# Layer 0's cross-attention: one weighted sum over two steps of scores instead of one per step, and where the third tile of exps is kept

## The chip, the cores and the metric

The kernel runs on one core of a Trainium2 chip. The metric is the device time of one execution in microseconds (us); lower is better. Five engines work side by side, each through its own list of instructions in order, and wait for each other by semaphores: TensorE (PE in the profile; its weight loads are listed apart as PEld), VectorE (DVE), ScalarE (ACT), GpSimd (POOL) and SyncE (SP), which here only starts transfers. TensorE writes its results to PSUM; VectorE and ScalarE read them from there.

## What is computed

The whole is a small network of two layers, each with a cross-attention, a second mixer and a feed-forward part. The change touches only the first cross-attention, with 2 sequences of 256 queries, 16 heads of width 16, and 4096 keys per sequence:

```python
def _L0_xattn_ref(x, z, Wq, Wkv, Wo):
    Q = (x @ Wq.T).reshape(B, xN, NUM_HEADS, HEAD_DIM)
    KV = (z @ Wkv.T).reshape(B, zN, 2, NUM_HEADS, HEAD_DIM)
    K = KV[:, :, 0]
    V = KV[:, :, 1]
    attn = jnp.einsum('bqhd,bkhd->bhqk', Q, K) * SCALE
    attn = jax.nn.softmax(attn, axis=-1)
    O = jnp.einsum('bhqk,bkhd->bqhd', attn, V).reshape(B, xN, DIM)
    return O @ Wo.T
```

The self-attention of layer 1, much later, uses two weight maps (`wq`, `wk`) whose place in memory moves with the change.

## The kernel before

All is in float32, which TensorE works off in two passes per matmul. The 16 heads of a sequence are cut into four groups of four heads; with two sequences there are eight groups `G`. The four heads of a group lie in four bands of 32 partitions, so that four score matmuls with 32 rows of contraction can run on TensorE at the same time, each on its own 32 rows of the array.

The softmax needs the largest score of each query, so a group is gone through twice, in 16 steps (`STEPS`) each:

- The first pass (function `first`) puts 128 queries on the partitions and 512 keys along the row, and VectorE takes the maximum along the row (`ve.reduce_max` in `scores`). After 16 steps `greatest` makes the maxima of the group final, and `lowered` writes them, negated, into a spare row of the queries, by a transpose on TensorE (`ps_negm`).
- The second pass (function `second`) puts 128 keys on the partitions and 256 queries along the row, for two blocks of keys per step, and ScalarE takes the exponential into `exps`, a tile in SBUF (`se.activation`).
- The weighted sum (function `weigh`) multiplies these exps with the values `V`. Here the array is used the other way, with 128 rows of contraction and 32 columns per head: four heads side by side on columns. A sum of a step is eight matmuls into one bank of PSUM (`av`), and VectorE adds that bank to an accumulator in SBUF (also named `av`).

The second pass of a group runs `LAG` = 17 steps behind its first pass, so in steps 17 to 127 one step holds both: the first pass of step `n` and the second pass of step `s = n - 17`. Such a step calls `scores` twice. Each call has eight matmuls: two heads of the first pass into one double tile of two banks (`banks`, a ring of two such tiles, `ps2`), and the other two heads of the second pass into two single banks (`bank`, a ring of four, `ps1`). The sums, the keys (`ps_k`), the values (`ps_v`), the transposes of the maxima and the final transposes of a group (`ps_o`, in `finished`) take their banks from the same ring of four. After the two calls comes `weigh` for the step before, and after that what `made` has laid down for this step: every fourth step the projection of another 512 keys and, in most of the stage, of 512 values.

In steps 0 to 16 only the first pass runs, in steps 128 to 144 only the second, mixed there with the first instructions of the next stage.

`in_order` makes the instructions of the engines stand in the order in which the program calls them; from step 17 on nothing is moved by the scheduler within an engine. Loads that are not urgent (`LATE`) are issued on GpSimd's queue, one entry per step from step 20.

The exps live in one tile of 4096 columns (tag `P`), used in two halves in turn (`s % 2`). The maps `a1_wq` and `a1_wk` have tiles of their own, loaded through `LATE`.

Of the kernel before, what the change touches and what calls it, by code (L numbers as in the profile page):

```python
# [10 lines left out]
F32 = mybir.dt.float32  # L11
# [4 lines left out]
P = 128  # L16
B, NQ, D = 2, 256, 256
# [6 lines left out]
E, FF = 8, 1024  # L24
# [18 lines left out]
def perceiver(ctx: ExitStack, tc: tile.TileContext, d: dict, out: bass.AP):  # L43
    nc = tc.nc
# [5 lines left out]
    big = ctx.enter_context(pool("big", 1))  # L50
# [4 lines left out]
    def bank(name):  # L55
        return ps1.tile([P, 512], F32, tag="bank", name=name)
# [7 lines left out]

    def large(tag, name):
        return big.tile([P, 4096], F32, tag=tag, name=name)

# [25 lines left out]
    for j in range(4):  # L95
        nc.gpsimd.memset(one0[32 * j : 32 * j + 1, :], 1.0)
    ctxT = [large(f"ctx{b}", f"ctxT{b}") for b in range(B)]

    def load_ctxT(b, c, eng):
# [6 lines left out]
    load_ctxT(0, 2, nc.sync)  # L106
    load_ctxT(0, 3, nc.sync)
    cols = const.tile([P, 2, d["cols"].shape[1]], F32, tag="cols", name="cols")
    wo0, bcw, gate_w, out_w, x1_wq, x1_wkT, x1_wv, a1_wq, a1_wk, a1_wv, a1_wo, wr = (
        const.tile([P, d[n].shape[0] // P, d[n].shape[1]], F32, tag=n, name=n)  # L110
        for n in (
            "l0_wo", "l0_bcw", "l0_gate_w", "l0_out_w", "x1_wq", "x1_wkT", "x1_wv",
            "a1_wq", "a1_wk", "a1_wv", "a1_wo", "moe_wr",
        )
    )
    bcb = const.tile([P, 2 * NS], F32, tag="l0_bcb", name="l0_bcb")
# [15 lines left out]
    def ctxT1(c):  # L132
# [4 lines left out]
        late(t, (t, d[n].rearrange("(c p) n -> p c n", p=P)))  # L137
        for t, n in (
            (wo0, "l0_wo"), (bcw, "l0_bcw"), (gate_w, "l0_gate_w"), (out_w, "l0_out_w"), (cols, "cols"),
            (x1_wq, "x1_wq"), (x1_wkT, "x1_wkT"), (x1_wv, "x1_wv"), (a1_wq, "a1_wq"), (a1_wk, "a1_wk"),  # L140
            (a1_wv, "a1_wv"), (a1_wo, "a1_wo"), (wr, "moe_wr"),
        )
    ] + [
# [531 lines left out]
    def self_attention(b, bank):  # L675
# [138 lines left out]
        for n in range(NG + 3):  # L814
# [20 lines left out]
            if 0 <= n - 3:  # L835
                weigh(n - 3, pe(n - 3))
# [27 lines left out]
    with pool("l0x", 1) as one:  # L864
# [19 lines left out]
        STEPS = NK // 2  # L884
# [14 lines left out]
        def blank(i, c):  # L899

            nc.scalar.copy(KB[i][:, c * 1024 : (c + 1) * 1024], one0.to_broadcast([P, 1024]))

        KC = {}

        def keys(h2, c):

            b, half = divmod(h2, 2)
            ps = bank("ps_k")
            te.matmul(
                ps, lhsT=wkc[:, half * P : (half + 1) * P], rhs=ctxT[b][:, c * 512 : (c + 1) * 512],  # L910
                start=True, stop=True,
            )
            KC[h2, c] = KCS[(h2 * chunks + c) % 4]
            se.copy(KC[h2, c], ps)
# [69 lines left out]
        def scores(n, ms, s, ss, p):  # L984


            work, done = [], []
            for j, pair in ms:
                G, i = divmod(n, STEPS)
                c, qt = divmod(i, 2)  # L990
                tiles, at = homes(pair)
                work += [(first, n, j + jj, at[jj]) for jj in range(2)]
                for k, t in enumerate(tiles):
                    w = 2 // len(tiles)
                    done.append(
                        lambda t=t, o=MP[G][:, qt, j + k : j + k + w, c]: ve.reduce_max(o, t, axis=AX.X)
                    )
            for j, pair in ss:
                tiles, at = homes(pair)
                work += [(second, s, j + jj, at[jj]) for jj in range(2)]  # L1000
                for k, t in enumerate(tiles):
                    w = 2 // len(tiles)
                    o = p[:, j + k : j + k + w, :] if pair else p[:, j + k, :]
                    done.append(lambda t=t, o=o: se.activation(o, t, AF.Exp))
            for h in range(2):
                for f, *at in work:
                    f(*at, h)
            for f in done:
                f()

        def weigh(n, p):

            G, kp = divmod(n, STEPS)
            b, g = groups[G]
            vt = VT[2 * b + g // 2]
            ps = bank("av")
            for c in range(2):
                for j in range(4):
                    at = (2 * kp + c) * HW + (4 * (g % 2) + j) * VW
                    te.matmul(  # L1020
                        ps[32 * j : 32 * j + 32, :NQ],
                        lhsT=vt[:, at : at + 32],
                        rhs=p[:, j, c * NQ : (c + 1) * NQ],
                        start=(c == 0),
                        stop=(c == 1),
                    )
            if kp == 0:
                AV[G] = one.tile([P, NQ], F32, tag="av", name="av")
                ve.tensor_copy(AV[G], ps[:, :NQ])
            else:  # L1030
                ve.tensor_tensor(AV[G], AV[G], ps[:, :NQ], ALU.add)

        def greatest(G):
            m = small.tile([P, 2, 4], F32, tag="m", name="m")
            ve.reduce_max(m, MP[G], axis=AX.X)
            lowest_of(lambda qt: m[:, qt, :], negm)

        def lowered(G):
            b, g = groups[G]
            lower(QT[g][:, b * NQ : (b + 1) * NQ], negm, bank("ps_negm"))  # L1040

        def finished(G):
            b, g = groups[G]
            ps = bank("ps_o")
            for qt in range(2):
                te.transpose(ps[:, qt * P : (qt + 1) * P], AV[G][:, qt * P : (qt + 1) * P], ident)
            o = ps[:, : 2 * P].rearrange("p (q j r) -> p q j r", q=2, r=32)
            f = small.tile([P, 2, 4], F32, tag="af", name="f")
            ve.reciprocal(f, o[:, :, :, DH])
            ve.tensor_tensor(  # L1050
                O[b][:, :, 4 * DH * g : 4 * DH * (g + 1)].rearrange("p q (j r) -> p q j r", r=DH),
                o[:, :, :, :DH],
                f.unsqueeze(3).to_broadcast([P, 2, 4, DH]),
                ALU.mult,
            )
# [34 lines left out]
            f(*at)  # L1090
        for c in range(4):
            blank(1, c)
        before = None
        closing = None
        for n in range(NM + LAG + 1):
            G, i = divmod(n, STEPS)
            s = n - LAG
            one_pass = n < NM
            other = 0 <= s < NM
            if s == 0:  # L1100
                exps = large("P", "exps")
            p = exps[:, s % 2 * 2048 : (s % 2 + 1) * 2048].rearrange("p (j n) -> p j n", j=4) if other else None
            if one_pass and i == 0:
                MP[G] = small.tile([P, 2, 4, NC // 512], F32, tag="mp", name="mp")
            in_order[0] = other
            if one_pass and other:
                scores(n, [(2, True)], s, [(0, False)], p)
                if i == 0:
                    lowered(G - 1)
                scores(n, [(0, True)], s, [(2, False)], p)  # L1110
            else:
                four = [(2, False), (0, True)]
                if one_pass:
                    scores(n, four, s, [], p)
                elif other:
                    scores(n, [], s, four, p)
                if n and i == 0 and n <= NM:
                    lowered(G - 1)
            if one_pass and i == STEPS - 1:
                greatest(G)  # L1120
            if closing is not None:
                finished(closing)
                closing = None
            if before:
                weigh(*before)
            if before and before[0] % STEPS == STEPS - 1:
                closing = before[0] // STEPS
            before = (s, p) if other else None
            for f, *at in made.get(n, ()):
                f(*at)  # L1130
        if closing is not None:
# [28 lines left out]
        weights.append((w1, w2))  # L1160

    LOADED = len(HOMES)
    xn5 = const.tile([P, NT, D], F32, tag="l0_wq", name="xn5")
    count = const.tile([P, P], F32, tag="l0_wv", name="count")
    nc.gpsimd.iota(count, pattern=[[1, P]], base=1, channel_multiplier=0, allow_small_or_imprecise_dtypes=True)
# [36 lines left out]
    for stream in streams.values():  # L1202
        assert next(stream, None) is None
    for e in range(LOADED):
        experts(e)
# [3 lines left out]
    with pool("ffn", 1) as one:  # L1209
# [83 lines left out]
        two = one.tile([P, TOP_E, NT, E], F32, tag="two", name="two")  # L1293
# [6 lines left out]
        for t in range(NT):  # L1300
            for i in range(TOP_E):
                w = nc.gpsimd.indirect_dma_start(
                    out=x_slots, out_offset=bass.IndirectOffsetOnAxis(ap=at[:, i, t : t + 1], axis=0),
                    in_=xn5[:, t, :], in_offset=None,
# [7 lines left out]
        before = one.tile([P, E - 1, E], F32, tag="before", name="before")  # L1312
# [140 lines left out]
        def next_weights(k):  # L1453
            e = k + LOADED
            if e < ALWAYS:
                experts(e if e < E else expert_of(e))
            if k == STORED - 3:
                shares(STORED)
                shares(STORED + 1)
            if k == STORED - 1:  # L1460
                collect()
# [109 lines left out]
```

## Time and profile before

| | us |
|---|---|
| median of three runs | 868.06 (865.57 to 869.98) |
| the profiled execution | 865.26 |
| its span, first to last instruction | 863.5 |

The profile is of one execution. Its span is 1.8 us shorter than the time of the same execution, and that time is 2.8 us under the median. Most lines of the kernel go through the class `Engine`, so the profile shows them all as line 164, and one has to tell them apart by the names of their tiles: `mp<-ps` are the maxima of the first pass, `exps<-ps` the exponentials of the second, `av<-exps,V` the weighted sums, `av<-av` their additions. In a row of a matmul a count is of passes, two per matmul. "x4" behind a line of the timeline means four instructions merged into one line.

The stage with both passes runs from about 67 us to 445 us. Cut into stretches, engine by engine (busy us, number of instructions), its middle looks the same throughout:

```profile
240.00:280.00 40.00, 40.00 (x582) 26.81 (x582) 30.79 (x35) 27.52 (x53) 0.00 (x0) 1.00 0.08 19
280.00:320.00 40.00, 39.86 (x566) 26.58 (x563) 31.32 (x41) 25.87 (x51) 0.59 (x2) 1.00 0.09 19
320.00:360.00 40.00, 39.96 (x584) 26.85 (x584) 31.51 (x40) 26.44 (x51) 0.00 (x0) 1.00 0.10 22
```

The columns after the stretch and its length are TensorE, its weight loads, VectorE, ScalarE and GpSimd, then the granted clock of TensorE as a share of full speed, the share of the DMA engines and GB/s.

### The profile page before, as it was taken

To read this page: it belongs to the slowest core of one execution; us is meant where nothing else is said; L and a number is where in the kernel's file an instruction comes from. 1 tells how busy PE (TensorE), PEld (TensorE's weight loads), DVE (VectorE), ACT (ScalarE), POOL (GpSimd) and SP (SyncE) were. 2 spreads that over 40 slices of the span, in tenths; PEclk is the share of its full clock that TensorE was granted. 3 is DMA by queue.
4 is the path that set the end of the run, shared out by engine and by line. 5 is a ranking of instruction groups with operands and counts; after the bars stand their busy time and mean duration, and the time that the engine had idled before them with its cause. 6 is when DMAs were issued, how large, how long until landed. Compare 5 with 4: busy or idle time off the path is not lost.

```text
span 863.5 us, 20999 instructions
## 1 busy us (share of the span) xinstructions
PE 814.6 (94%) x8640; PEld 586.5 (68%) x8640; DVE 571.9 (66%) x1044; ACT 458.8 (53%) x858; POOL 46.1 (5%) x108
## 2 busy tenths in 40 slices
PE   5999999999999999999999899878999999699996
PEld 3665666666666666666665478756488866499995
DVE  4788888878787878788863668985743376641112
ACT  6436666766666666666668758621642225411120
POOL 5004020000000000000000000000000000030003
PEclk9999999999999999999999989998999969889999
DMA  7216131011010010000010203000222500529602
GB/s 269 55 32 184 24 115 42 21 23 23 17 23 20 19 23 19 22 19 2 2 51 2 80 19 86 13 1 1 97 98 98 195 1 2 195 70 329 229 20 81
DMA packets 35314, 56.67 MB, mean 66 GB/s; under 512 B 5872, under 2 KB 22816, under 8 KB 35216
## 3 DMA queue, kind: packets, MB, share of 16 engines
q1 hardware_dynamic: 27904, 41.44, 15.8%
q0 software_dynamic: 3264, 10.05, 3.6%
q10 hardware_dynamic: 4048, 3.80, 1.5%
q8 instruction: 70, 1.15, 0.6%
q14 instruction: 28, 0.23, 0.1%
HBM read 42.16 MB, written 4.85 MB: 54 GB/s over the span
## 4 chain that ended last, share of the span: by engine, by line
PE 83%; DVE 8%; ACT 4%; issue 2%; DMA 1%; POOL 1%; ACTq 0%; POOLq 0%; DVEq 0%
PE ps L164 29%; PE av L164 17%; PE ps_h L1362 5%; PE ps_y L1378 4%; PE ps_s L164 4%; DVE states L164 4%; PE ps_k L164 4%; PE ps_v L164 3%; PE ps_aqk L164 2%; PE ps_am L164 2%; PE ps_pt L164 1%; PE ps_ht L164 1%; PE asc L164 1%; PE ps_q L164 1%; PE ps_f L164 1%
## 5 line engine op out<-in xcount | busy, mean ns | idle before, releaser
L164 DVE TENSOR_REDUCE mp<-ps 128x2 f32<-128x1024 f32 (+1 forms) x273 | 302.6, 1153 | 88.4 <-PE ps L164 88.4
L164 ACT ACTIVATE exps<-ps 128x512 f32<-128x512 f32 (+1 forms) x495 | 263.8, 617 | 111.4 <-PE ps L164 111.1
L164 PE MATMUL ps<-qk,KB 32*128 32x256 f32 x2048 | 250.0, 392 | 1.7 <-DVE qk L164 1.7
L164 PE MATMUL ps<-KB,qk 32*128 32x256 f32 x2048 | 244.8, 390 | 0.0
L164 PEld LDWEIGHTS ps<-KB,qk 32*128 32x128 f32 x2048 | 172.1, 184 | 52.6 <-issue 37.7
L164 PEld LDWEIGHTS ps<-qk,KB 32*128 32x128 f32 x2048 | 183.9, 184 | 13.2 <-issue 4.8
L164 PE MATMUL av<-exps,V 128*32 128x256 f32 x2048 | 137.9, 387 | 2.7 <-DVE more L164 1.6
L164 PEld LDWEIGHTS av<-exps,V 128*32 128x32 f32 x2048 | 53.9, 109 | 66.4 <-ACT exps L164 37.9
L164 DVE TENSOR_TENSOR av<-av 128x256 f32<-128x256 f32 x120 | 49.4, 412 | 20.4 <-PE av L164 20.4
L1369 ACT ACTIVATE room<-ps_h 128x512 f32<-128x512 f32 x24 | 14.2, 597 | 72.5 <-PE ps_h L1362 60.3
L1362 PEld LDWEIGHTS ps_h<-room,w 128*128 128x128 f32 x384 | 44.5, 192 | 0.5
L1362 PE MATMUL ps_h<-room,w 128*128 128x128 f32 x384 | 44.8, 275 | 0.0
L164 DVE TENSOR_TENSOR_SCAN states<-decay,ps_in 128x256 f32<-128x256 f32 x64 | 39.7, 667 | 5.4 <-PE ps_in L164 5.4
L1378 PE MATMUL ps_y<-w,room 128*128 128x256 f32 x192 | 43.3, 379 | 0.0
L164 PEld LDWEIGHTS ps_v<-l_wv,ctxT 128*128 128x128 f32 x256 | 32.6, 191 | 15.4 <-issue 6.3
L1378 PEld LDWEIGHTS ps_y<-w,room 128*128 128x128 f32 x192 | 35.6, 190 | 4.4
L164 PE MATMUL ps_v<-l_wv,ctxT 128*128 128x128 f32 x256 | 35.0, 280 | 1.2 <-ACT V L164 1.2
L164 PE MATMUL ps_k<-ctxT,wkc 128*128 128x512 f32 x64 | 35.5, 640 | 0.0
L164 PE MATMUL av<-more,nat 128*128 128x256 f32 x128 | 32.9, 381 | 0.3 <-ACT more L164 0.3
L164 ACT COPY qk<-ps_k 128x512 f32<-128x512 f32 x32 | 18.6, 587 | 25.5 <-PE ps_k L164 25.5
L164 ACT ACTIVATE states<-states,more 128x256 f32<-128x256 f32 x64 | 28.2, 498 | 6.6 <-PE ps_in L164 5.9
L164 ACT ACTIVATE aexps<-asc 128x512 f32<-128x512 f32 x32 | 17.0, 604 | 24.7 <-PE asc L164 24.7
(302 smaller groups left out, 901.1 us busy)
## 6 DMA issues: line engine op xcount, KB each, us to landing
w<-in_moe_w SPq DMA_DIRECT2D x24, 1024.0 KB, 7.7
KB<-qk SPq DMA_DIRECT2D x220, 32.0 KB, 2.0
ctxT<-in_ctxT SPq DMA_DIRECT2D x4, 512.0 KB, 8.0
ctxT<-in_ctxT POOLq DMA_DIRECT2D x4, 512.0 KB, 6.3
x_slots<-O POOLq DMA_DIRECT2D x15, 128.0 KB, 6.4
y_slots<-room ACTq DMA_DIRECT2D x10, 128.0 KB, 3.5
room<-x_slots ACTq DMA_DIRECT2D x9, 128.0 KB, 5.0
KB<-qk ACTq DMA_DIRECT2D x32, 32.0 KB, 2.0
```

The lines of the kernel that those rows point to most:

```text
L164: i = getattr(self.engine, name)(*args, **kw)
L1362: nc.tensor.matmul(ps[fc // 4][:, (fc % 4) * P : (fc % 4 + 1) * P], lhsT=weights[k][0][:, c, fc * P : (fc + 1) * P], rhs=xT[k][:, c, :], s ...
L1369: nc.scalar.activation(hT[k][:, 4 * i : 4 * i + 4, :].rearrange("p f n -> p (f n)"), ps[i], AF.Silu)
L1378: nc.tensor.matmul(ps[:, :D], lhsT=hT[k][:, fc, :], rhs=weights[k][1][:, fc, :], start=(fc == 0), stop=(fc == NF - 1),)
```

## The change

The sum of two steps in a row is now one accumulation of sixteen matmuls in one bank, done behind the scores of every second step (even `s`), over the exps of steps `s - 2` and `s - 1`. VectorE adds that bank to the accumulator once for two steps. The scores of the step `s` itself are written while the exps of the two steps before are still wanted, so a third tile of exps is needed: `exps_of` gives the two halves of tag `P` and a new tile of 2048 columns with tag `E` in turn (`s % 3`). To make room for it, `a1_wq` and `a1_wk` lose their tiles and share that new tile's place; they are loaded into it on GpSimd's queue after the loop.

```diff
-    wo0, bcw, gate_w, out_w, x1_wq, x1_wkT, x1_wv, a1_wq, a1_wk, a1_wv, a1_wo, wr = (
+    wo0, bcw, gate_w, out_w, x1_wq, x1_wkT, x1_wv, a1_wv, a1_wo, wr = (
...
-            (x1_wq, "x1_wq"), (x1_wkT, "x1_wkT"), (x1_wv, "x1_wv"), (a1_wq, "a1_wq"), (a1_wk, "a1_wk"),
+            (x1_wq, "x1_wq"), (x1_wkT, "x1_wkT"), (x1_wv, "x1_wv"),
...
+        EXPS = []
+
+        def exps_of(s):
+
+            if not EXPS:
+                two = large("P", "exps")
+                third = big.tile([P, 2048], F32, tag="E", name="exps")
+                EXPS.extend((two[:, :2048], two[:, 2048:], third))
+            return EXPS[s % 3].rearrange("p (j n) -> p j n", j=4)
...
-        def weigh(n, p):
+        def weigh(n, ps_of):
...
-            for c in range(2):
+            for c in range(4):
                 for j in range(4):
                     at = (2 * kp + c) * HW + (4 * (g % 2) + j) * VW
                     te.matmul(
                         ps[32 * j : 32 * j + 32, :NQ],
                         lhsT=vt[:, at : at + 32],
-                        rhs=p[:, j, c * NQ : (c + 1) * NQ],
+                        rhs=ps_of[c // 2][:, j, c % 2 * NQ : (c % 2 + 1) * NQ],
                         start=(c == 0),
-                        stop=(c == 1),
+                        stop=(c == 3),
                     )
...
-            if before:
-                weigh(*before)
-            if before and before[0] % STEPS == STEPS - 1:
-                closing = before[0] // STEPS
-            before = (s, p) if other else None
+            if s > 0 and s % 2 == 0:
+                weigh(s - 2, before)
+                before = []
+                if s % STEPS == 0:
+                    closing = s // STEPS - 1
+            if other:
+                before.append(p)
...
+    maps = big.tile([P, 2048], F32, tag="E", name="a1_wqk").rearrange("p (i c n) -> p i c n", i=2, c=2)
+    a1_wq, a1_wk = maps[:, 0, :, :], maps[:, 1, :, :]
+    for t, n in ((a1_wq, "a1_wq"), (a1_wk, "a1_wk")):
+        nc.gpsimd.dma_start(out=t, in_=d[n].rearrange("(c p) n -> p c n", p=P))
```

More of the change, by code (lines that the diff above doesn't have):

```diff
@@ L108, in perceiver @@
     cols = const.tile([P, 2, d["cols"].shape[1]], F32, tag="cols", name="cols")
-    wo0, bcw, gate_w, out_w, x1_wq, x1_wkT, x1_wv, a1_wq, a1_wk, a1_wv, a1_wo, wr = (
+    wo0, bcw, gate_w, out_w, x1_wq, x1_wkT, x1_wv, a1_wv, a1_wo, wr = (
         const.tile([P, d[n].shape[0] // P, d[n].shape[1]], F32, tag=n, name=n)
         for n in (
-            "l0_wo", "l0_bcw", "l0_gate_w", "l0_out_w", "x1_wq", "x1_wkT", "x1_wv",
-            "a1_wq", "a1_wk", "a1_wv", "a1_wo", "moe_wr",
+            "l0_wo", "l0_bcw", "l0_gate_w", "l0_out_w", "x1_wq", "x1_wkT", "x1_wv", "a1_wv", "a1_wo", "moe_wr",
         )
@@ L1092, in perceiver @@
             blank(1, c)
-        before = None
+        before = []
         closing = None
@@ L1099, in perceiver @@
             other = 0 <= s < NM
-            if s == 0:
-                exps = large("P", "exps")
-            p = exps[:, s % 2 * 2048 : (s % 2 + 1) * 2048].rearrange("p (j n) -> p j n", j=4) if other else None
+            p = exps_of(s) if other else None
             if one_pass and i == 0:
@@ L1123, in perceiver @@
                 closing = None
-            if before:
-                weigh(*before)
-            if before and before[0] % STEPS == STEPS - 1:
-                closing = before[0] // STEPS
-            before = (s, p) if other else None
+            if s > 0 and s % 2 == 0:
+                weigh(s - 2, before)
+                before = []
+                if s % STEPS == 0:
+                    closing = s // STEPS - 1
+            if other:
+                before.append(p)
             for f, *at in made.get(n, ()):
```

## The prediction

> **What bounds the kernel now.** I read the page first: TensorE is busy 94% of the span, and the chain that ended last lies 83% on it, 29% in the score tiles (`ps`) and 17% in the groups named `av`, nearly all of them weighted sums of layer 0 (the cross-attention of layer 1 uses the same name). The groups of instructions then give counts and durations.
>
> ```profile
> span 863.5 us, 20999 instructions
> PE 814.6 (94%) x8640; PEld 586.5 (68%) x8640; DVE 571.9 (66%) x1044; ACT 458.8 (53%) x858; POOL 46.1 (5%) x108
> ...
> L164 DVE TENSOR_REDUCE mp<-ps 128x2 f32<-128x1024 f32 (+1 forms) x273 | 302.6, 1153 | 88.4 <-PE ps L164 88.4
> L164 ACT ACTIVATE exps<-ps 128x512 f32<-128x512 f32 (+1 forms) x495 | 263.8, 617 | 111.4 <-PE ps L164 111.1
> ...
> L164 PE MATMUL av<-exps,V 128*32 128x256 f32 x2048 | 137.9, 387 | 2.7 <-DVE more L164 1.6
> ...
> L164 DVE TENSOR_TENSOR av<-av 128x256 f32<-128x256 f32 x120 | 49.4, 412 | 20.4 <-PE av L164 20.4
> ```
>
> The averages hide the stage that is changed, so I went to the timeline of two plain steps there (start, duration, engine, work; the bracket is idle time before it).
>
> ```profile
> 308.91 0.19 PEld L164 LDWEIGHTS ps<-KB,qk 32*128 32x128 f32 x2 [0.41 <-issue]
> ...
> 310.10 2.36 DVE L164 TENSOR_REDUCE mp<-ps 128x2 f32<-128x1024 f32 x2 [0.26 <-PE ps L164]
> ...
> 310.20 2.06 ACT L164 ACTIVATE exps<-ps 128x512 f32<-128x512 f32 x4 [0.88 <-PE ps L164]
> ...
> 310.95 0.59 PEld L164 LDWEIGHTS av<-exps,V 128*32 128x32 f32 x16 [0.33 <-ACT exps L164]
> ...
> 311.95 0.19 PEld L164 LDWEIGHTS ps<-KB,qk 32*128 32x128 f32 x2 [0.41 <-issue]
> ...
> 312.37 0.41 DVE L164 TENSOR_TENSOR av<-av 128x256 f32<-128x256 f32 x1
> ...
> 313.13 2.36 DVE L164 TENSOR_REDUCE mp<-ps 128x2 f32<-128x1024 f32 x2 [0.35 <-PE ps L164]
> ...
> 313.89 0.59 PEld L164 LDWEIGHTS av<-exps,V 128*32 128x32 f32 x16 [0.33 <-ACT exps L164]
> ...
> 314.89 0.19 PEld L164 LDWEIGHTS ps<-KB,qk 32*128 32x128 f32 x2 [0.41 <-issue]
> ```
>
> A step begins at 308.91, the next at 311.95, the third at 314.89: 5.98 us for two. TensorE never rests in it, but VectorE is nearly full too: two maxima and one addition fill all but 0.26 to 0.35 us of each 2.94 to 3.04.
>
> Two smaller readings are needed: how long one maximum holds its tile, and how late TensorE starts on a result of VectorE.
>
> ```profile
> 284.00 1.22 DVE L164 TENSOR_REDUCE mp<-ps 128x2 f32<-128x1024 f32 x1
> ...
> 66.82 0.41 DVE L164 TENSOR_TENSOR qk<-qk,ps_negm 128x256 f32<-128x256 f32 x1
> ...
> 67.38 0.48 PE L164 MATMUL ps<-qk,KB 32*128 32x256 f32 x2 [1.67 <-DVE qk L164]
> ```
>
> One maximum takes 1.22 us, but the next starts about 1.14 after it (the addition at 312.37 starts 2.27 after the first of two maxima at 310.10). From 66.82 + 0.41 = 67.23 to 67.38 TensorE needed 0.15 us.
>
> **What the Trainium skill says.** *TensorEngine Tiling (Array Packing)*, Key Properties: a change of tiling mode drains TensorE. The trace agrees: inside a score group the rounds of four concurrent passes follow at 0.2133 us (309.24, 309.45, 309.67, 309.88 in the timeline), but the four rounds of the sum (0.85) take 1.00 until the scores begin, and the round before the sum and the first one after it take some 0.1 more each. The step of 2.94 us less its 12 rounds (2.56) gives 0.38 us for the round trip; the steps of 3.04 hold a further 0.1, a wait for the bank of the last sum. The same page, PSUM Bottleneck, says that tiling speeds TensorE and not the evacuation of PSUM. Here VectorE's maximum of 1.22 us stands against 0.85 us of TensorE for the tile that it empties. *Perfetto Trace Analysis*, Optimizing Scalar/DVE Operations, says that a part of the profiled latency overlaps with the next instruction; the 1.22 against 1.14 agrees.
>
> **The change, part by part.** Call the half steps of two steps A1, B1, A2, B2, and the sum W. Each half writes a double tile for VectorE (`banks`, two in all) and two single banks for ScalarE (`bank`, four in all). Before: A1 B1 W A2 B2 W. After: A1 B1 A2 B2 W, with W twice as long. The instruction order of the two kernels agrees: sixteen matmuls of a sum stand after 32 of scores, and the first matmul of each half waits for VectorE.
>
> *Removed:* one round trip between modes in two steps, 0.38 us of TensorE, and one addition, 0.41 us of VectorE. TensorE's own work for two steps is then 24 rounds of 0.2133 = 5.12 plus 0.38 = 5.50 us. That would be 0.48 less than 5.98.
>
> *Added, a wait:* the sum of the odd step was also what TensorE did while VectorE emptied the double tiles. Without it A2 comes at once, and needs the tile that A1 filled. I count from the first weight load of A1 (time 0), by the intervals of the trace:
> - A1's maximum starts at 1.18 (310.10 is 1.19 after 308.91; 313.13 is 1.18 after 311.95) and ends at 2.40. B1's starts at 2.32 and ends at 3.54.
> - TensorE is through with A1 and B1 at 1.85. A2 waits for 2.40 + 0.14 = 2.54: 0.69 lost.
> - A2's four rounds go to 3.39. B2 needs B1's maximum: 3.54 + 0.14 = 3.68: 0.29 lost.
> - The last of B2's rounds starts 0.64 later and W 0.31 after that: 4.63.
> - W takes 1.00 + 4 x 0.2133 = 1.85, so the next A1 is at 6.48.
>
> Everything behind the wait (all of A2, B2, W, and the next pair's scores) moves, since TensorE works in order. VectorE can't catch up: after B2's maximum (about 5.97) it finds nothing but the one addition until the next A1 is ready at 6.48 + 1.18. So 6.48 replaces 5.98: 5.50 + 0.69 + 0.29, a loss of 0.98 against a gain of 0.48. *Net +0.51 us per plain pair.* ScalarE isn't next: eight exps at 0.515 (2.06 for four) are 4.1 us; the first two end at about 2.4, and A2's banks are free in time. The third tile of exps is enough too: W has read both old tiles before the exps that overwrite them can start.
>
> *How many pairs:* steps 18 to 127 run both passes, 55 pairs. Keys and values come behind W, every fourth step, before and after: a pair with both takes 7.92 instead of 5.98 now, and keeps that surplus. Six pairs hold the transposed maxima (`ps_negm`) between A1 and B1, which gives VectorE time; now such a pair takes 3.99 + 2.94 = 6.93, and after I get 6.90 (the wait for A1's exps before B1 is there in both): taken as 0, upper end 0.25. Six pairs hold `ps_o` between B1 and A2. It would hide in the 0.69, but it takes a bank of the ring, so that a score of A2 waits for B1's exps and one of B2 for VectorE's reading of `ps_o`: between 0 and 0.45 a pair, taken as 0.2. So 43 x 0.51 = 21.9, plus 1.2, is +23.1.
>
> *The second pass alone* (steps 128 to 144) has no maxima. A step takes 2.08 to 2.20 us, and ScalarE's exps 2.04 (4.08 for two), so a round trip saved is worth about 0.1 a step; half of the additions go too, which wait behind long reciprocals of the next stage near 482 to 492. The last W comes 0.85 later in full. I take -1.5, between -5 and +1.
>
> *Maps loaded later:* two loads of 512 KB in the POOL queue, 4.0 and 5.7 us to land before. They now stand behind the last W, near 500, on DMA engines that are 20% busy there, and are needed by the self-attention at 675. In that queue only memsets of that stage follow. Nothing. If the cover of 170 us were gone, it would be 10 us. The six later entries of that list move up two steps, and are needed long after: nothing.
>
> Sum: 865.26 us (the profiled execution; its span is 863.5) + 21.6 = 886.9. The median of the runs shown, 868.06, is 2.8 higher, which would give 889.7. I say 888.
>
> **Rivals.**
> 1. *The drain saved and no wait* (the change's gain alone): 55 pairs less 0.48 is -26, so 839. For it: TensorE is at 94%, and its rounds are what the chain of waits shows. Against it: the double tile is held 1.22 us by each maximum, and the order of instructions has a wait for VectorE on every half. It decides from where the two lost pieces (0.98) fall under 0.48: for that each maximum and its signal would have to be some 0.25 us shorter. Chance 0.06.
> 2. *The wait just eats the gain:* the same price near 0.5, when part of the signal's delay lies under the weight loads: 866 to 870. Chance 0.04.
> 3. *More is lost:* the bank of W is emptied at 7.31 by the addition, and B1's second bank is that one, wanted at 7.46; one more delay of 0.1 to 0.2 in each pair, with the ring shifted by `ps_k` and `ps_v`, and the full 0.45 at `ps_o`: +33, so 900. For it: today's wait of that kind is the 0.1 that separates steps of 2.94 and 3.04. Against: the margin of 0.15 holds. Chance 0.12.
> 4. *The forecast:* 0.78.
>
> **How the numbers follow.** In the forecast the delay of 0.14 may be 0.05 to 0.2, once in each cycle: -5 to +3. The two unknowns at `ps_o` and `ps_negm` give -1 to +3, the last steps -3.5 to +2.5. With these it runs from 880 to 896; reaching some way into 2 and 3, the range is 876 to 899. A difference of 0.5% (4.3 us) is about what a measurement of this kernel can tell. Faster 0.07, same 0.03, slower 0.90.
>
> **What would show it.** In the changed kernel's timeline: steps of about 2.5 and 3.95 us in turn; idle time of TensorE before a score group with VectorE's maximum as its releaser, about 1 us per pair; a gap on VectorE of 0.9 between the last maximum and the addition; one `av` block of 1.85. The count of additions falls from 120 to 56. I am wrong if A2 follows B1 at 0.2 us, or if the pair takes 5.5.

## The result, and the profile after

The changed kernel takes 894.07 us (median of four runs, 892.56 to 896.73) against 867.9 us (865.57 to 869.98, four runs) before: 1.0306 times as long, with a 95% interval of 1.0266 to 1.0345. The loss of 26.2 us is a little more than the 21.6 of the forecast. The profiled executions lie 4.1 us further apart than the medians: 895.54 us (span 893.8) against 865.26 (863.5).

First the page of the changed kernel: the same two rows of VectorE as before, and between them one row of weight loads and one of sums.

```profile
span 893.8 us, 20855 instructions
...
L164 DVE TENSOR_REDUCE mp<-ps 128x2 f32<-128x1024 f32 (+1 forms) x273 | 303.1, 1154 | 96.7 <-PE ps L164 92.1
...
L164 PEld LDWEIGHTS ps<-KB,qk 32*128 32x128 f32 x2048 | 170.7, 185 | 88.2 <-DVE mp L164 57.4
...
L164 PE MATMUL av<-exps,V 128*32 128x256 f32 x2048 | 126.1, 386 | 0.8 <-ACT exps L164 0.8
...
L164 DVE TENSOR_TENSOR av<-av 128x256 f32<-128x256 f32 x56 | 23.6, 421 | 49.4 <-PE av L164 48.4
```

No work was added: the maxima are the same 273, and the additions fell from 120 to 56. What is new stands behind the bar: the weight loads of the scores were idle for 57.4 us until a maximum (`mp`) was done. (Idle time is counted from the end of the load before, so a part of each wait is the usual distance between loads and not lost.) In the list of waits of the kernel before, that entry was 2.5 us:

```profile
PEld ps L164 <- DVE mp L164: 2.5, 6, 0.4
```

And in the list of the changed kernel (total us, times, longest):

```profile
PEld ps L164 <- DVE mp L164: 57.4, 98, 0.9
```

The timeline of one plain pair of steps of the changed kernel shows where these waits are.

```profile
332.38 0.19 PEld L164 LDWEIGHTS ps<-KB,qk 32*128 32x128 f32 x2 [0.41 <-issue]
332.52 0.42 DVE L164 TENSOR_TENSOR av<-av 128x256 f32<-128x256 f32 x1 [0.67 <-PE av L164]
333.56 4.82 DVE L164 TENSOR_REDUCE mp<-ps 128x2 f32<-128x1024 f32 x4 [0.62 <-PE ps L164]
333.67 2.06 ACT L164 ACTIVATE exps<-ps 128x512 f32<-128x512 f32 x4 [1.85 <-PE ps L164]
334.84 0.19 PEld L164 LDWEIGHTS ps<-KB,qk 32*128 32x128 f32 x2 [0.85 <-DVE mp L164]
335.98 0.19 PEld L164 LDWEIGHTS ps<-KB,qk 32*128 32x128 f32 x2 [0.39 <-DVE mp L164]
336.13 2.22 ACT L164 ACTIVATE exps<-ps 128x512 f32<-128x512 f32 x4 [0.40 <-PE ps L164]
337.05 1.45 PEld L164 LDWEIGHTS av<-exps,V 128*32 128x32 f32 x32 [0.33 <-ACT exps L164]
```

The pair starts at 332.38. A1 and B1 run through, by 1.85 us after the start. A2's weights are loaded at 334.84 (2.46 after the start) behind A1's maximum, B2's at 335.98 (3.60) behind B1's, and the sum begins at 337.05 (4.67). The four maxima follow each other without a gap, and then VectorE has nothing to do for 0.67 us before the addition and 0.62 us after it. The sum before this one began at 330.52, so the pair takes 6.53 us, against 5.98 before.

To compare kernels by stage I use the small reduction that ends a group's first pass (`m<-mp`). There are eight of them, and the time from the first to the last is nearly the whole stage with both passes. In the kernel before it runs from 64.01 to 445.73 us (381.7), in the changed one from 65.39 to 475.10 (409.7). Of the 30.3 us between the two spans, this stage has 28.0. The start has 1.4, the steps without maxima up to `ps_bct` have 1.4 (445.73 to 493.61 before, 475.10 to 524.43 after), and the rest of the kernel is 0.5 faster. The 1.4 of the start can't be put down to the change: two variants of the changed kernel below, with the same work up to there, reach the first of these reductions at 64.35 and 64.83 us. Of the stage, the first group has more than its part (56.42 us against 51.88, 4.5 more, where a steady group has 3.9 more). From 60 to 80 us the granted clock of TensorE was 0.94 and then 0.89 in this execution, and 1.00 in that of the kernel before, which may be the reason. One steady group of 16 steps, or eight pairs, takes 57.0 us before and 60.9 after. That group time is used for the experiments below, beside the whole time.

### The profile page after: what moved, and what is told of

The parts are those of the page before. It is cut to its first block, busy times and chain, and to the rows that moved or that the text cites. A ratio compares the mean times of both kernels' runs of the same rounds, so it can differ in the third digit from the quotient of the medians.

```text
span 893.8 us, 20855 instructions
## 1 busy us (share of the span) xinstructions
PE 824.4 (92%) x8640; PEld 589.0 (66%) x8640; DVE 556.4 (62%) x980; ACT 464.4 (52%) x858; POOL 46.1 (5%) x106
## 4 chain that ended last, share of the span: by engine, by line
PE 77%; DVE 15%; ACT 4%; issue 2%; DMA 1%; POOL 1%; ACTq 0%; POOLq 0%; DVEq 0%
PE ps L164 26%; PE av L164 16%; DVE mp L164 7%; PE ps_h L1377 5%; PE ps_y L1393 4%; PE ps_s L164 4%; DVE states L164 4%; PE ps_k L164 3%; PE ps_v L164 3%; PE ps_am L164 2%; PE ps_aqk L164 2%; PE ps_q L164 1%; PE ps_pt L164 1%; PE ps_ht L164 1%; PE asc L164 1%
## 5 line engine op out<-in xcount | busy, mean ns | idle before, releaser
L164 ACT ACTIVATE exps<-ps 128x512 f32<-128x512 f32 (+1 forms) x495 | 269.3, 614 | 115.0 <-PE ps L164 112.5
L164 PE MATMUL ps<-KB,qk 32*128 32x256 f32 x2048 | 262.2, 397 | 19.9 <-DVE mp L164 19.4
L164 PE MATMUL ps<-qk,KB 32*128 32x256 f32 x2048 | 264.1, 397 | 3.8 <-DVE qk L164 1.8
L164 PEld LDWEIGHTS ps<-KB,qk 32*128 32x128 f32 x2048 | 170.7, 185 | 88.2 <-DVE mp L164 57.4
L164 PEld LDWEIGHTS ps<-qk,KB 32*128 32x128 f32 x2048 | 176.5, 185 | 15.1 <-ACT exps L164 5.5
L164 PE MATMUL av<-exps,V 128*32 128x256 f32 x2048 | 126.1, 386 | 0.8 <-ACT exps L164 0.8
L164 PEld LDWEIGHTS av<-exps,V 128*32 128x32 f32 x2048 | 60.2, 110 | 56.5 <-ACT exps L164 20.5
L164 DVE TENSOR_TENSOR av<-av 128x256 f32<-128x256 f32 x56 | 23.6, 421 | 49.4 <-PE av L164 48.4
L164 ACT COPY V<-ps_v 128x512 f32<-128x512 f32 x32 | 18.8, 586 | 22.2 <-PE ps_v L164 17.0
```

The source lines that it names most:

```text
L164: i = getattr(self.engine, name)(*args, **kw)
```

## The experiments

The ratio of a run is to runs of the kernel before that were made together with it; their medians are 867.65 to 868.4 us.

Theory: with the sum only behind every second step, three halves of scores follow another half directly. The second and third of them wait until their PSUM tiles have been emptied, and behind the doubled sum the emptying engine runs dry. Rivals: the long accumulation itself, its single bank, or the loads that were moved.

| run | median us | ratio to before (95%) | us per steady group |
|---|---|---|---|
| before | 867.9 | | 57.0 |
| changed | 894.07 | 1.0306 (1.0266 to 1.0345) | 60.9 |
| changed, half maxima | 881.02 | 1.0152 (1.0109 to 1.0194) | 59.3 |
| before, half maxima | 859.41 | 0.9888 (0.9861 to 0.9915) | 56.4 |
| changed, two sums apart | 897.66 | 1.0336 (1.0304 to 1.0367) | 60.9 |
| before, maps and third tile only | 867.81 | 1.0000 (0.9983 to 1.0016) | 57.0 |
| changed, half maxima and half exps | 852.61 | 0.9820 (0.9792 to 0.9849) | 55.4 |
| before, half maxima and half exps | 857.5 | 0.9877 (0.9836 to 0.9918) | 56.0 |
| changed, half exps only | 894.6 | 1.0302 (1.0273 to 1.0332) | 60.9 |
| changed, sum in the middle of the second step | 901.33 | 1.0364 (1.0312 to 1.0417) | 61.2 |
| before, sum between the halves | 870.3 | 1.0015 (1.0000 to 1.0030) | 56.8 |

### The maxima made shorter

The suspected wait is shortened at its source (the line is shown without the `lambda` around it).

```diff
-  ve.reduce_max(o, t, axis=AX.X)
+  ve.reduce_max(o, t[:, :, :256] if len(t.shape) == 3 else t[:, :256], axis=AX.X)
```

In the changed kernel:

> The changed kernel with each first-pass maximum taken over half of its columns (the second 256 of every 512 keys are left out of the maximum, so the shift of the softmax is lower; scores, exps and sums are all there). Theory (TensorE waits in the second step of a pair for VectorE to empty the two double tiles): a maximum takes about 0.7 us in place of 1.22, so A1's is done at about 1.9 and B1's at about 2.8 us from the start of the pair, where TensorE wants the tiles at 1.85 and 2.7; both waits nearly vanish, the pair falls from 6.53 to 5.5 to 5.7 us, and the kernel from 894 to about 840 to 852 us. Rival (the longer sum, its bank, or the later steps cost the time, not the maxima): no change beyond 5 us, 889 to 895.

In the kernel before:

> The kernel before with the same half maxima (the second 256 of every 512 keys are left out of the maximum). Theory (before, TensorE never waits for a maximum in this stage): only the 0.1 us that VectorE's late addition costs in every second step can go, so 861 to 868 us, and the changed kernel with half maxima is 12 to 25 us faster than this one: the saved change of tiling mode, 0.35 to 0.45 us in each of 55 pairs. Rival (VectorE bounds both kernels alike): this one falls by as much as the changed one does, by 40 us or more.

The changed kernel fell by 13 us to 881.02, which is neither the 840 to 852 of my theory nor the standstill of the rival. The timeline of the second step of a pair in the changed kernel with half maxima says why:

```profile
322.18 0.19 PEld L164 LDWEIGHTS ps<-KB,qk 32*128 32x128 f32 x2 [0.32 <-DVE mp L164]
...
322.68 0.18 PEld L164 LDWEIGHTS ps<-qk,KB 32*128 32x128 f32 x1 [0.19 <-ACT exps L164]
...
324.71 1.45 PEld L164 LDWEIGHTS av<-exps,V 128*32 128x32 f32 x32 [0.33 <-ACT exps L164]
```

Now the exponentials end a wait, 0.5 us after the maxima did, and the pair still takes 6.32 us (this sum begins at 324.71, the one before it at 318.39). In the list of waits ScalarE, the second emptying engine with its ring of four single banks, now stands beside VectorE for the score tiles. In the changed kernel its entry was 5.5 us:

```profile
PEld ps L164 <- ACT exps L164: 15.6, 68, 0.8
PEld ps L164 <- DVE mp L164: 14.5, 44, 0.8
```

VectorE ended the waits, but taking it away uncovers ScalarE only 0.2 us below. In the kernel before the steps of 3.04 us became steps of 2.94, as expected. It took 859.41 us, a little below the 861 to 868 of the expectation. The other half of that expectation was wrong: the changed kernel with half maxima was not 12 to 25 us faster than this one, but 21.6 us slower.

### The sum left in two, at its new place

```diff
-                weigh(s - 2, before)
+                for at in before:
+                    weigh(*at)
```

with `weigh` as it was before the change: eight matmuls, one bank and one addition for each step.

> The changed kernel with the two sums kept apart, eight matmuls into one bank and eight into another, one addition each, but both behind the second step's scores as in the change. Theory (where the sum stands costs the time, not that it is one accumulation): 6.53 to 6.65 us per pair, 893 to 900 us. Rival (the long accumulation in one bank, or the single addition late behind it, costs the time): back to 866 to 880 us.

It took 897.66 us, and a group of 60.9 us, the same as the changed kernel's. So in the stage with both passes neither the accumulation over sixteen matmuls nor the merged addition costs or saves anything that counts. The time goes with the place of the sums. The whole is 3.6 us longer than the changed kernel, outside the steady groups; the cause of that was not followed up.

### The memory part alone

Three tiles of exps in turn, and the maps loaded after the loop, with `weigh` once per step as before.

> The kernel before with only the memory part of the change: three tiles of exps in turn, and the two maps of the self-attention loaded after the loop into the third tile's place; one sum per step as before. Theory (that part is hidden: the maps are wanted some 150 us after they land): 866 to 870 us, no difference. Rival (the late loads or the third tile cost part of the 26 us): 872 us or more.

867.81 us, a ratio of 1.0000: that part is hidden.

### Both emptying engines shortened

The exponentials are cut to the first of a step's two key blocks, and the tiles of exps are set to zero once.

```diff
+  o, t = (o[:, :, :256], t[:, :, :256]) if pair else (o[:, :256], t[:, :256])
   done.append(lambda t=t, o=o: se.activation(o, t, AF.Exp))
```

In the changed kernel, with half maxima as well:

> The changed kernel with half maxima (as in the first run) and half exponentials too (the second of a step's two key blocks is left out of the exps; its place is zero, so these keys have no weight; their scores and products are still formed). Theory (the pair waits for whichever of VectorE and ScalarE empties its PSUM tiles last; with half maxima ScalarE's four single banks were next, 0.2 us behind): with both halved TensorE alone sets the pair, 5.5 to 5.65 us, and the kernel takes 833 to 848 us. Rival (something else holds the pair at about 6.3): 870 us or more.

In the kernel before, with the same two halves:

> The kernel before with half maxima and half exponentials (the same parts left out). Theory (TensorE with two changes of mode per step sets it): 2.94 us per step as with half maxima alone, 852 to 861 us; the changed kernel with the same halves is 12 to 24 us faster than this one, so that the saved change of mode is seen free of waits. Rival (a saved change of mode is worth nothing): the two are equal.

In the changed kernel, with half exponentials only:

> The changed kernel with half exponentials only (the second key block of each step is left out of them), the maxima whole. Theory (VectorE's maxima end the waits of the changed kernel, ScalarE only comes next): the pair stays at 6.5 us, only the last steps without maxima may gain: 886 to 894 us. Rival (ScalarE's banks hold the pair): 870 to 882 us, as with the half maxima.

The order is reversed: with both engines shortened the changed kernel takes 852.61 us and the kernel before 857.5. The ranges of the two (851.84 to 853.35 and 854.5 to 860.39) don't overlap. So the saved change of mode is real, and what buries it is the time in which the tiles are emptied. With the exponentials alone shortened nothing happens (894.6 us, just above the 886 to 894 expected, and 60.9 per group): VectorE still holds the pair. Each engine would hold it alone, and both must be faster.

The gain was smaller than I expected, 5 us in place of 12 to 24, and the time was above my 833 to 848. A plain pair takes 5.79 us (303.19 to 308.98 from sum to sum), not 5.5 to 5.65, against 5.88 in the kernel before with the same halves. The timeline of the changed kernel with both halves shows what is left:

```profile
328.25 0.19 PEld L164 LDWEIGHTS ps<-KB,qk 32*128 32x128 f32 x2 [0.32 <-DVE mp L164]
...
328.57 0.19 PEld L164 LDWEIGHTS ps<-KB,qk 32*128 32x128 f32 x2
...
330.24 1.45 PEld L164 LDWEIGHTS av<-exps,V 128*32 128x32 f32 x32 [0.33 <-ACT exps L164]
```

A wait of 0.3 us behind A1's maximum remains, although that maximum takes only 0.69 us now. The pair started at 326.32. Its scores up to the sum take 3.92 us, where 16 rounds without a wait would take 3.65 (one step's 1.94 and eight rounds more of 0.2133). The saved 0.38 us less this 0.27 leaves 0.11 us in a pair, and 0.09 is what the pairs differ by. Where the wait is absent, nearly all of the saving is seen: in the pair with the transposed maxima (`ps_negm`) no score load waits for a maximum, and it takes 6.37 us (330.24 to 336.61) against 6.72 in the kernel before with the same halves (334.11 to 340.83). The stage of these two kernels differs by 5.75 us (374.7 against 368.95), a steady group by 0.7; 1.5 of the 5.75 lie in the first group and were not taken apart.

### The sum in the middle of the second step

`weigh` is called between the two calls of `scores` of the even step: A1 B1 A2 W B2.

> The changed kernel with the sum of two steps moved between the two halves of the second step's scores (A1 B1 A2 W B2). Theory (only two double tiles: wherever one block of 1.85 us stands, three of the four halves come in a row and wait for maxima of 1.2 us, and VectorE runs dry behind the block): by the same recurrence 6.4 to 6.6 us per pair, 888 to 897 us. Rival (it is enough that the sum covers one of the two waits): 0.3 us per pair less, 874 to 882 us.

In its timeline two sums of plain pairs begin so:

```profile
331.69 1.45 PEld L164 LDWEIGHTS av<-exps,V 128*32 128x32 f32 x32 [0.33 <-ACT exps L164]
...
338.22 1.45 PEld L164 LDWEIGHTS av<-exps,V 128*32 128x32 f32 x32 [0.33 <-ACT exps L164]
```

That is 6.53 us, to the digit the pair of the changed kernel. The whole time is above my range (901.33, runs from 896.62 to 904.8), and the trace shows two reasons. A steady group is 0.3 us longer, and that lies in the pair with the transposed maxima: 7.46 us from sum to sum (300.37 to 307.83) against 6.94 in the changed kernel. The pairs with keys and values are even a little shorter (8.42 against 8.48). B2 now stands behind the sum, so a group's last maximum comes late, and the transposition waits for it. First this run, then the changed kernel:

```profile
305.25 0.41 PE L164 MATMUL ps_negm<-ident,negm 128*128 128x128 f32 x2 [1.00 <-DVE negm L164]
...
302.56 0.44 PE L164 MATMUL ps_negm<-ident,negm 128*128 128x128 f32 x2
```

The rest lies ahead of the steady groups (60.2 us for the first one, 56.4 in the changed kernel). There the granted clock of TensorE was lower in this execution: 0.84 from 60 to 70 us and 0.65 from 70 to 80, where the changed kernel had 0.94 and 0.89. An estimate from these shares gives 3.4 of the 3.8 us. The four runs of this kernel agree: the one with the highest mean clock (0.981) took 896.62 us, the one with the lowest (0.963) 904.8.

### A version meant to beat both

One sum per step, but between the halves (A W B), over the exps of two steps earlier, with the third tile and the late maps of the change. Keys and values follow the sum; those of the second sequence come one step later, and the late loads' markers read another column of the maxima.

> The kernel before, one sum of eight matmuls per step, but standing between the two halves of a step's scores (A W B), over the exps of two steps earlier, for which the third tile of exps and the late maps of the change are used; keys, values and the late loads' markers follow the sum. Theory (cover must be spread: with a sum between every second half TensorE never waits for a maximum, and the addition stands ahead of B's maximum, so that the small wait for the last sum's bank in every second step goes): 2.94 us per step in place of 2.94 and 3.04 in turn, 859 to 866 us. Rival (the place of a sum doesn't matter while there is one per step): 866 to 870 us.

A miss: 870.3 us, which is what the rival said, and steps of 2.94 and 3.04 us in turn, as before. Its timeline has the addition where it was, behind two maxima:

```profile
311.39 2.36 DVE L164 TENSOR_REDUCE mp<-ps 128x2 f32<-128x1024 f32 x2 [2.30 <-PE ps L164]
...
312.15 0.59 PEld L164 LDWEIGHTS av<-exps,V 128*32 128x32 f32 x16 [0.33 <-ACT exps L164]
...
313.67 0.41 DVE L164 TENSOR_TENSOR av<-av 128x256 f32<-128x256 f32 x1
...
315.19 0.59 PEld L164 LDWEIGHTS av<-exps,V 128*32 128x32 f32 x16 [0.33 <-ACT exps L164]
```

The reason is plain afterwards. Repeated, A W B A W B is the same ring as A B W A B W with the halves renamed: two halves, one sum. The sum in the middle of the second step is the same case: four halves, one sum. In the plain steps only the number of halves between two sums is left to matter, and neither run changes it.

One test is missing. A ring of three double tiles would change the number of tiles itself. That two are too few rests on the order of the program (A2 writes the tile that A1 filled) and on the releasers in the trace, not on a run.

## Why the prediction was right

- *The mechanism.* A2 waits for A1's maximum, B2 for B1's, and VectorE runs dry behind W: seen in the timeline at the places forecast, and tied to the emptying of the tiles by the five runs with shortened maxima or exps. The signs of the forecast are there: steps of 2.46 and 4.07 us in turn (forecast 2.5 and 3.95), idle time with the maximum as releaser, one `av` block of 1.86 us, 56 additions. Only the gap on VectorE ahead of the addition is 0.67 us and not 0.9. The forecast let the addition begin some 0.4 us after the sum, as it does in the kernel before. But there it stands behind two maxima (at 312.37, right at their end); free of them it begins 0.14 us after the sum (332.52 after 332.38). So the bank of the sum came free earlier than the third rival reckoned.
- *The plain pair.* Forecast 6.48 us, measured 6.53. Two terms were off and nearly cancelled. The signal from VectorE to TensorE was taken as 0.14 us; A1's maximum ends about 334.78 (333.56 + 1.22) and the weights load at 334.84, which is 0.06. On the other side I gave a half after a wait rounds of 0.2133 us throughout. Its first round takes 0.32, as after a change of mode, so from B2's first load to the sum it is 1.07 us and not 0.95.
- *The pairs with `ps_o`.* Of the terms per pair this one was mis-sized most. Taken as 0.2 us, bounds 0 to 0.45; measured 0.55 (8.95 us from sum to sum where it was 8.40, keys and values in both). In six pairs that is 2 us more.
- *The pairs with `ps_negm`.* Taken as 0; 6.94 us after against 6.93 before.
- *The stage.* 43 x 0.55 + 6 x 0.55 is 27, and the time from the first to the last group differs by 28.0; the surplus of the first group, told above, is most of the rest. Forecast 23.1.
- *The second pass alone.* Forecast -1.5, between -5 and +1; measured +1.4 up to `ps_bct`, and the last sum included about +1 (the kernel after it is 0.5 faster). Of all terms this one is furthest off, and its sign was wrong. The claim that a saved change of mode is worth 0.1 us per step there was wrong. Two plain steps take 4.28 us before (455.11 to 459.38, 459.38 to 463.66) and 4.28 after (488.11 to 492.39). In the changed kernel the second half of the sum waits for exps that ScalarE is only just finishing:

```profile
490.05 0.59 PEld L164 LDWEIGHTS av<-exps,V 128*32 128x32 f32 x16 [0.33 <-ACT exps L164]
...
491.39 0.59 PEld L164 LDWEIGHTS av<-exps,V 128*32 128x32 f32 x16 [0.75 <-ACT exps L164]
```

  What makes up the 1.4 us there was not taken apart.
- *Maps and third tile at nothing.* Right, by the run with that part alone.
- *"ScalarE isn't next."* Right in that it didn't hold the changed kernel, as the run with half exps alone shows. But it stands 0.2 us behind VectorE, and so my first rival's point of decision (each maximum 0.25 us shorter) was wrong. Maxima 0.5 us shorter left the changed kernel at 881.02 against 859.41 for the kernel before with the same maxima.

## What to carry to other kernels

A piece of work that needs no PSUM tile of the contended ring (the sum here needs none of the double tiles) is also the time in which the other engines empty that ring. Before merging two such pieces to save a switch, count how many tiles the ring holds and how long the slowest reader keeps one: here a saving of 0.48 us per plain pair (0.38 for the change of mode, 0.1 for a wait that went with it) cost 1.03 us of waits. And look for the next reader behind the first, since a wait that is shortened may only fall to the second one. Moving a block within a repeated cycle changed nothing in the plain steps of two runs, where the sequence, read as a ring, stayed the same.

## What the runs showed that I had not expected

A wait for a tile costs TensorE more than the time by which the tile is late. In the timelines here a weight load begins one round of matmuls ahead of its own. When the first load of a half is held, it starts together with its matmul, and the second round follows at 0.32 us and not at 0.21. From the timeline of the changed kernel, the first and second round of A2:

```profile
319.83 0.48 PE L164 MATMUL ps<-KB,qk 32*128 32x256 f32 x2 [0.45 <-DVE mp L164]
...
320.15 0.38 PE L164 MATMUL ps<-KB,qk 32*128 32x256 f32 x2
```

The weight load was due at 318.99, with the last round of B1 and one round ahead of the matmul due at 319.21. So a tile has to be free some 0.2 us earlier than its matmul suggests, and being late costs another 0.11. That is most of what was left of the loss when both emptying engines were shortened: there A2 began 0.10 us late (328.25, due at 328.15), and its second round 0.11 later still, together 0.21 of the 0.27 us.
